# Gated cross attention with a Sinkhorn-mixed feed-forward: the output mask spread over the partitions by a product instead of a transfer, and three more chunks of mixing moved behind the last residual

## The chip, the cores and the metric

One Trainium2 chip, one core of it. The metric is the device time of one execution in microseconds (us). PE is TensorE, DVE is VectorE, ACT is ScalarE, POOL is GpSimd; SP's queue issues most of the transfers, ACT's queue some stores.

## The reference

The inputs are x and a context of shape (8, 512, 2048), 32-bit floats, and a mask of shape (8, 1, 2048) (all ones in the inputs drawn, but read by the kernel as data). The computation has two gated residual steps:

```
x = x + tanh(g_xattn) * xattn(layernorm(x), ctx, mask)
x = x + tanh(g_ffn)   * ffn(layernorm(x))

xattn: the 2048 columns are cut into 16 patches of 128 columns
  q, k = Wq, Wk @ layernorm(x) + bias      (256 x 128 per patch, 8 heads of 32)
  v    = Wv @ ctx + bias
  attn = softmax(q k / sqrt(32), masked)   within the patch
  o    = gelu(attn v)
  out  = (Wo @ o + bo) * mask

ffn: each row of 2048 is 4 streams of 512
  logits = rmsnorm(row) @ W.T + base       (24 of them: 16, 4 and 4)
  H_res  = 50 Sinkhorn iterations on the 4x4 matrix, mixed with the identity by a gate
  H_pre, H_post = softmax of 4 each
  y      = (sum_n H_pre[n] stream[n]) @ W_branch
  out[i] = sum_j H_res[i, j] stream[j] + H_post[i] * y
```

The mask multiplies the whole output of the attention, the bias `bo` included. The kernel uses that Wo is linear: it multiplies the mask into `o` ahead of Wo, and adds mask times `bo` as one more product.

## The kernel before

**Blocks and steps.** A batch has 512 rows; its 2048 columns are cut into 4 blocks of 512 columns, 32 blocks over the 8 batches. A block is 4 patches, and the loop runs over patches, `t` from 0 to 131, with `n = t // 4` the block. In each step a string, `ORDER`, gives the order in which parts are put into the program: `e` exponentials, `a` attention times v, `g`, `o` and `O` the output of the block before (`outp`), `p` and `P` the q/k projection of two blocks ahead, `s` scores and their maxima, `v` the v projection, `S` the statistics, `M` mixing. The program is written for a scheduler that lays out each engine's instructions by the order in which they are written (an earlier place is a higher priority) and by when their inputs and buffers come free in its own model of time; so an instruction can stand ahead of where it was written if its inputs are ready, and then the order on each engine is fixed.

**The output of a block (`outp`).** Its first part applies the gelu to `o` (L665, ACT, between two loads of an activation table, L665 and L667), loads the mask of the block's columns to all 128 partitions (`mb`, L669, one transfer of 256 KB on SP's queue with a single row as source, in a pool with one buffer), and multiplies `o` by it on POOL (L670). The second part transposes `o` on PE (L679), copies (L680), and forms the products that the logits need (L683); loads six rows of the mask's parts to `MR` (L691); and splits `o` into a high and a low part (`gh` L693 on ACT, `gl` L695 on POOL). The third part forms Wo times `o` in four row groups of 128 (L705 to L707), each closed by the product that adds mask times bias:

```python
T.matmul(ps, bo6[:, cs], mr, start=False, stop=True)
```

and adds the residual (L709, DVE), a sum of squares (L711, ACT), and a store of the new x to the tensor `x1s` in HBM (L712).

**The mask in three parts.** A 32-bit float is the sum of three bf16 numbers, each the rounded rest of the one before (`split3`). The mask's three parts and the bias's three parts stand in six rows each, `mrow_d` (and from it the two tiles `MR`, filled with zeros below the six rows) and `bo6`, paired so that the product over the rows gives the six leading terms of mask times bias.

**The chain of a batch.** When a batch's four blocks are done, `rawmap` and `ffn` make its logits and run the Sinkhorn iterations, 49 sweeps of small instructions (L882 to L892) that alternate between DVE and POOL (for the last batch DVE alone). For batches that have chunks on PE, `ffn` also writes small tensors to HBM and reads them back in another layout: `rec` (L834, L836) and `HR` (L923, L925).

**Two forms of mixing.** A batch's output is made in four chunks of 128 rows. `mixv` does a chunk on ACT, DVE and POOL: it loads the four streams (L953), forms the branch input (L958, L962, L963), transposes it and multiplies by W_branch on PE (L943 to L945), and for each of the four output streams adds up scaled streams (L981, L985, L986, L988) and the branch (L991), with a store on SP's queue (L992). `mixp` does a chunk by products: it loads the same rows interleaved (L1009), adds the mean on ACT (L1011), forms the branch input with a block-diagonal weight `PD` (L1012), transposes, multiplies by W_branch (L943 to L945 again, to `yp`), and forms the outputs by two products each with weights built on POOL from `post` and `HR` (`QD`, L1035 and L1036; L1046 and L1047), ending in a copy on ACT (L1049) and a store on ACT's queue (L1050).

The table `PE_MIX` says which chunks of each batch take the second form. Chunks of the first form go to the queue `mixq`, which is worked off within the loop, 3.25 steps of a chunk's 13 per loop step, from 30 steps after the batch's chain was written; batch 4's from t = 113 on. Chunks of the second form go to `tailq`, which is written behind the whole loop, so behind the residual of block 31. Before the change `tailq` holds 12 chunks: one of batch 4, four each of batches 5 and 6, three of batch 7.

**Buffers around the change.** `mb` has one buffer. `MR` are two tiles, taken in turn. PSUM is three pools of two buffers each: `ps_s` for scores, `ps_p` for projections, v, Wo and parts of `mixp`, `ps_t` (tag `t`) for attention times v, transposes, statistics and branch results.

Of the kernel before, what the change touches and what calls it, by code (L numbers as in the profile page):

```python
# [9 lines left out]
F32 = mybir.dt.float32  # L10
F32R = mybir.dt.float32r
F16 = mybir.dt.float16
BF16 = mybir.dt.bfloat16
# [6 lines left out]
P = 128  # L20
# [5 lines left out]
BLK = 512  # L26
# [48 lines left out]
D_OUT = 0  # L75
D_ST = 0
BUF_XP = 10
PE_MIX = ((), (), (), (), (3,), (0, 1, 2, 3), (0, 1, 2, 3), (1, 2, 3))
SPLITS = (1, 1, 1, 1, 1, 1, 1, 1)
CHAINS = ((0,), (1,), (2,), (3,), (4,), (5,), (6,), (7,))  # L80
BUF_SK = 2
# [17 lines left out]
def gated_xattn_mhc_kernel(  # L99
# [21 lines left out]
    V, A, G, T, SY = nc.vector, nc.scalar, nc.gpsimd, nc.tensor, nc.sync  # L121
# [6 lines left out]
    def ctile(shape, dt, name):  # L128
        return const.tile(shape, dt, tag=name, name=name)
# [27 lines left out]
    bor = ctile([3, 512], F32R, "bor")  # L157

    bo6 = ctile([P, 512], BF16, "bo6")
    MR = [ctile([P, BLK], BF16, f"MR{i}") for i in range(2)]  # L160
    cs3 = ctile([3, 2], F32, "cs3")
    base_t = ctile([P, NM], F32, "base_t")
# [10 lines left out]
    mrow_d = dram.tile([6, B * S], BF16, tag="mrow_d", name="mrow_d")  # L173
# [22 lines left out]
    ps_t = ctx.enter_context(tc.tile_pool(name="ps_t", bufs=2, space=PSUM))  # L196
# [166 lines left out]
    with tc.tile_pool(name="set", bufs=1) as st:  # L363
# [7 lines left out]
        def split3(parts, a, shape, name):  # L371

            left = stile(shape, F32, name)
            V.tensor_copy(parts[:, 0, :], a)
            V.tensor_tensor(left, a, parts[:, 0, :], ALU.subtract)
            V.tensor_copy(parts[:, 1, :], left)
            V.tensor_tensor(parts[:, 2, :], left, parts[:, 1, :], ALU.subtract)
# [97 lines left out]

        mh = stile([B * 16, 3, P], BF16, "mh")
        split3(mh, mkt, [B * 16, P], "mks")
        for r, t in enumerate((0, 0, 1, 0, 1, 2)):
            SY.dma_start(mrow_d[r : r + 1, :].rearrange("o (k w) -> (o k) w", w=P), mh[:, t, :])
        mT = ptile(B * 16, "mT")  # L480
        T.transpose(mT, mkt, ident[: B * 16, : B * 16])
# [23 lines left out]
        with ExitStack() as behind:  # L505
            for i in last.values():
                behind.enter_context(tc.issue_after(i.ins))

            wo = stile([P, 2, 512], F32, "wo", "w2")
            SY.dma_start(wo, woT.rearrange("(c p) d -> p c d", p=P))  # L510
            V.tensor_scalar(wo, wo, tgx, None, ALU.mult)
            A.copy(WoH, wo)
            V.tensor_tensor(WoL, wo, WoH.bitcast(F32), ALU.subtract)
            bo32 = stile([1, 512], F32, "bo32")
            SY.dma_start(bo32, bo.rearrange("(o e) -> o e", o=1))
            V.tensor_scalar(bo32, bo32, tgx[0:1, :], None, ALU.mult)
            boh = stile([1, 2, 512], F32R, "boh")
            V.tensor_copy(boh[:, 0, :], bo32)
            V.tensor_tensor(boh[:, 1, :], bo32, boh[:, 0, :].bitcast(F32), ALU.subtract)
            for t, r in ((0, 0), (1, 1), (0, 2)):  # L520
                SY.dma_start(brow_d[r : r + 1, :], boh[:, t, :].bitcast(F32))
            SY.dma_start(bor.bitcast(F32), brow_d)
            bo3 = stile([1, 3, 512], BF16, "bo3")
            split3(bo3, bo32, [1, 512], "bos")
            for t in [bo6] + MR:
                V.memset(t, 0.0)
            for r, t in enumerate((0, 1, 0, 2, 1, 0)):
                SY.dma_start(bo6[r : r + 1, :], bo3[:, t, :])


            V.memset(Wm, 0.0)
            V.memset(Wm[:, :, NM : NM + 1], 1.0)
            SY.dma_start(Wm[:, :, 0:NM], wmT.rearrange("(c p) m -> p c m", p=P))
            ws = ps_t.tile([P, BLK], F32, tag="t", name="ws")
            for k in range(16):
                T.matmul(ws[:, 0:32], onesb, Wm[:, k, :], start=(k == 0), stop=(k == 15))
            A.copy(wsum, ws[:, :NM])
            SY.dma_start(base_t, base.partition_broadcast(P))

            V.memset(cs3[:, 0:1], 1.0)  # L540
            V.tensor_copy(cs3[:, 1:2], ident[0:3, 2:3])
            V.tensor_tensor(cs3[:, 0:1], cs3[:, 0:1], cs3[:, 1:2], ALU.subtract)


            wbr = stile([P, 4, 512], F32, "wbr", "w4")
            SY.dma_start(wbr, wb.rearrange("(c p) e -> p c e", p=P))
            wmx = stile([P, 1], F32, "wmx")
            V.tensor_reduce(wmx, wbr.rearrange("p c e -> p (c e)"), AX.X, ALU.max, apply_absolute_value=True)
            wms = ps_t.tile([P, BLK], F32, tag="t", name="wms")[:, 0:1]
            T.matmul(wms, onesb, wmx, start=True, stop=True)  # L550
            V.tensor_scalar(ibw, wms, 1e-18, 1.0 / W_CAP, ALU.max, ALU.mult)
            sbw = stile([P, 1], F32, "sbw")
            V.reciprocal(sbw, ibw)
            V.tensor_scalar(wbr, wbr, sbw, None, ALU.mult)
            A.copy(WbH, wbr)
            V.tensor_tensor(WbL, wbr, WbH, ALU.subtract)
# [103 lines left out]
    def outp(n):  # L660

        b, k = divmod(n, NBLK)
        o = ob.pop(n)
        for g in range(2):
            gi = A.activation(o[:, g], o[:, g], AF.Gelu, bias=bvc[:, g : g + 1])  # L665
        with tc.issue_after(gi.ins), tc.high_priority():
            A.preload_act_table_set(EXP_SET)  # L667
        mb = gp.tile([P, BLK], F32, tag="mb", name="mb")
        SY.dma_start(mb, mask[b, k * BLK : (k + 1) * BLK].partition_broadcast(P))  # L669
        G.tensor_tensor(o, o, mb.unsqueeze(1).broadcast_to([P, 2, BLK]), ALU.mult)  # L670
        j0 = n * NP
        gt_ = op_.tile([P, NP, DK + 1], F32, tag="gT", name="gT")
        G.tensor_copy(gt_[:, :, DK], maskT[:, j0 : j0 + NP])
        yield
        for q in range(2):
            pt = ps_t.tile([P, 2, 2, P], F32, tag="t", name="gTp")
            for j in range(2):
                for e in range(2):
                    T.transpose(pt[:, j, e, :], o[:, e, (2 * q + j) * P : (2 * q + j + 1) * P], ident)  # L679
            V.tensor_copy(gt_[:, 2 * q : 2 * q + 2, 0:DK], pt.rearrange("p j e s -> p j (e s)"))  # L680
        g4 = ps_t.tile([P, DK + 1], F32, tag="t", name="g4")
        for p in range(NP):
            T.matmul(g4[32 * p : 32 * p + 32, :], Wm[:, k * NP + p, :], gt_[:, p, :], start=True, stop=True)  # L683
        if k == 0:
            g4s = lnp.tile([P, DK + 1], F32, tag="g4s", name="g4s", bufs=2)
            V.tensor_copy(g4s, g4)
            G4[b] = g4s
        else:
            V.tensor_tensor(G4[b], g4, G4[b], ALU.add)
        mr = MR[n % 2]  # L690
        SY.dma_start(mr[0:6, :], mrow_d[:, n * BLK : (n + 1) * BLK])  # L691
        gh = gp.tile([P, 2, BLK], F32R, tag="gh", name="gh")
        A.copy(gh, o)  # L693
        gl = gp.tile([P, 2, BLK], F32R, tag="gl", name="gl")
        G.tensor_tensor(gl, o, gh.bitcast(F32), ALU.subtract)  # L695
        if k == 0:
            sq2[b] = lnp.tile([P, 4, NBLK], F32, tag="sq2", name="sq2")
            x1s[b] = x1d.tile([D, S], F32, tag="x1s", name="x1s")
        xt = xtile.pop(n)
        yield  # L700
        for c in range(4):
            ps = ps_p.tile([P, BLK], F32, tag="p", name="op")
            cs = slice(c * P, (c + 1) * P)
            for e in range(2):
                T.matmul(ps, WoH[:, e, cs], gh[:, e], start=(e == 0), stop=False)  # L705
                T.matmul(ps, WoH[:, e, cs], gl[:, e], start=False, stop=False)  # L706
                T.matmul(ps, WoL[:, e, cs], gh[:, e], start=False, stop=False)  # L707
            T.matmul(ps, bo6[:, cs], mr, start=False, stop=True)  # L708
            V.tensor_tensor(xt[c], ps, xt[c], ALU.add)  # L709
            jk = fp.tile([P, BLK], BF16, tag="ph", name="junk2", bufs=BUF_PH)  # L710
            A.activation(jk, xt[c], AF.Square, bias=nmean[b][:, c : c + 1], accum_out=sq2[b][:, c, k : k + 1])  # L711
            defer(D_X1, "x1", lambda cs=cs, c=c: SY.dma_start(x1s[b][cs, k * BLK : (k + 1) * BLK], xt[c]))  # L712
            yield
# [39 lines left out]
    def ffn(bs):  # L753

        NT = 4 * len(bs)
        b = bs[-1]
        pe_mix = [PE_MIX[q - B] or PE_IN[q - B] for q in bs]
        tg = ""
# [170 lines left out]
    def mix(b, maps):  # L929
        E, cst, pre, prc, post, rec, HR = maps  # L930
        for c in range(4):
            if c in PE_IN[b - B]:
                yield from mixp(b, c, maps, True)
            elif c not in PE_MIX[b - B]:
                yield from mixv(b, c, maps)
# [148 lines left out]
    def act(c, t):  # L1084
# [55 lines left out]
        elif c == "O":  # L1140
# [3 lines left out]
            if n >= 1 and p == 3:  # L1144
                at("outp", run, og_[0])
                bb_, kk_ = divmod(n - 1, NBLK)
                if kk_ == NBLK - 1:
                    at("raw", rawmap, bb_)
                    p0 = tc.cur_priority
                    for grp in CHAINS:  # L1150
                        if grp[-1] == bb_ - B + 8:
                            grp = [q + B - 8 for q in grp if q + B - 8 >= 0]
                            res = at("chain", ffn, grp)
                            for q, maps in zip(grp, res):
                                mixq.append((t + LAGS[bb_], mix(q, maps)))
                                for c_ in PE_MIX[q - B]:
                                    tailq.append(mixp(q, c_, maps))
# [11 lines left out]

    nl = len(tailq) - len(PE_MIX[-1])  # L1170

# [62 lines left out]
```

## Time and profile before

| | before |
|---|---|
| median of 3 runs | 1668.7 us (1663.1 to 1676.0) |
| profiled execution | 1677.35 us, span 1675.5 us |
| PE busy | 1477.9 us (88%) |
| DVE busy | 1194.7 us (71%) |
| ACT busy | 1065.9 us (64%) |
| POOL busy | 821.3 us (49%) |
| granted PE clock, mean | 0.958 |
| HBM | 226.7 MB read, 101.2 MB written |

The profile is of one execution; a line number is that of the kernel before. "Busy" counts the time in which at least one instruction runs on the engine. PE's products overlap one another, so the mean time of a single product is longer than the time by which the next one follows. Where a view says what an engine waited for, it names the instruction whose end released it. Block 27's mask product (L670) starts at 1322.7, block 31's, the last, at 1478.9; the last residual's product is issued at 1491.9, and the first product of `mixp` at 1493.6.

### The profile page before, as it was taken

The numbers are of one execution on the slowest core, as the hardware profiler recorded it, in microseconds if no ns is written. First come the engines' busy times: TensorE is split into PE (matmuls) and PEld (weight loads), VectorE is DVE, ScalarE is ACT, GpSimd is POOL, SyncE is SP. The second block draws the span as 40 slices with busy tenths as digits, with TensorE's granted clock in tenths as the row PEclk, the third lists the DMA queues.
The fourth block names the chain that finished last, engine by engine and source line by source line (L and its number), as shares of the span: only waits on it lengthen the run. The fifth ranks groups of instructions, "written<-read, shape, count | busy, mean of one in ns | idle before, by whom it ended". The sixth has DMA issues, their size and how long they took to land.

```text
span 1675.5 us, 31675 instructions
## 1 busy us (share of the span) xinstructions
PE 1477.9 (88%) x10517; PEld 882.5 (53%) x10517; DVE 1194.7 (71%) x3552; ACT 1065.9 (64%) x1930; POOL 821.3 (49%) x1158
## 2 busy tenths in 40 slices
PE   4898999999999888889898898889889989789897
PEld 2544556656656554555555555555555556543333
DVE  7443434665776578777886789877988788877865
ACT  3357366767666766677578766687667767555454
POOL 2321323545454455546565745666667644643212
PEclk8999999999999999999899999999999989799999
DMA  5689786677678755886688765886567665234353
GB/s 190 172 240 256 236 268 194 188 236 247 173 209 236 228 168 178 233 256 195 177 241 252 227 188 165 245 251 190 183 173 212 193 176 145 98 122 152 109 169 122
DMA packets 257410, 330.53 MB, mean 197 GB/s; under 512 B 43543, under 2 KB 143191, under 8 KB 257246
## 3 DMA queue, kind: packets, MB, share of 16 engines
q1 hardware_dynamic: 249038, 315.59, 63.8%
q10 hardware_dynamic: 8208, 12.92, 2.1%
q8 instruction: 83, 1.36, 0.3%
q14 instruction: 81, 0.66, 0.1%
HBM read 226.71 MB, written 101.16 MB: 196 GB/s over the span
## 4 chain that ended last, share of the span: by engine, by line
PE 34%; DMA 20%; DVE 18%; ACT 11%; issue 8%; POOL 7%; SPq 1%; ACTq 0%; POOLq 0%; DVEq 0%
PE vp L336 4%; DMA xs<-in_x_dram 4%; DVE w L988 4%; DMA xTt<-in_xT_dram 3%; DMA QK<-qd 3%; PE qk L288 2%; PE qk L289 2%; PE op L705 2%; PE qk L290 2%; DMA out_dram<-w 2%; DVE smax L349 2%; PE op L706 2%; DMA xc<-x1s 2%; DMA x<-x1s 2%; PE smax L346 2%
## 5 line engine op out<-in xcount | busy, mean ns | idle before, releaser
L336 PE MATMUL vp<-Wv,ct 128*128 128x256 f32 x1024 | 249.8, 398 | 19.0 <-ACT VF L337 9.7
L336 PEld LDWEIGHTS vp<-Wv,ct 128*128 128x128 f32 x1024 | 201.6, 200 | 55.0 <-ACT VF L337 12.8
L888 POOL TENSOR_TENSOR W<-E,uv 128x64 f32<-128x64 f32 x343 | 117.8, 348 | 196.3 <-DVE uv L886 100.6
L288 PE MATMUL qk<-xh,WqkH 128*128 128x512 f16 x512 | 196.9, 385 | 8.9 <-DVE ev L295 6.0
L349 DVE TENSOR_REDUCE smax<-smax 128x8 f32<-128x1024 f32 x128 | 155.8, 1217 | 64.8 <-PE smax L346 62.8
L276 POOL TENSOR_TENSOR xl<-xn,xh 128x512 f16<-128x512 f32 x126 | 155.2, 1232 | 93.3 <-ACT xh L274 87.4
L988 DVE SCALAR_TENSOR_TENSOR w<-x,Et,w 128x512 f32<-128x512 f32 x180 | 181.4, 1009 | 26.4 <-POOL w L986 16.3
L289 PE MATMUL qk<-xl,WqkH 128*128 128x512 f16 x512 | 196.7, 384 | 3.9 <-POOL xl L276 3.9
L290 PE MATMUL qk<-xh,WqkL 128*128 128x512 f16 x512 | 196.3, 383 | 0.0
L882 POOL TENSOR_TENSOR W<-E,uv 128x64 f32<-128x64 f32 x308 | 106.9, 352 | 176.1 <-DVE uv L892 80.2
L635 ACT ACTIVATE e<-sT,ebi,esc 128x1024 f32<-128x1024 f32 x128 | 153.2, 1197 | 35.4 <-PE sT L633 35.0
L271 POOL TENSOR_SCALAR xn<-xt,ln_r,nb 128x512 f32<-128x512 f32 x126 | 109.3, 868 | 112.2 <-DMA xt<-in_x_dram 51.9
L890 DVE TENSOR_REDUCE sm<-W 128x16 f32<-128x64 f32 x392 | 98.6, 255 | 71.0 <-POOL W L888 67.5
L705 PE MATMUL op<-gh,WoH 128*128 128x512 f32 x256 | 118.6, 465 | 24.3 <-DVE ev L295 11.4
L711 ACT ACTIVATE junk<-xt,nmean 128x512 bf16<-128x512 f32 x128 | 91.6, 715 | 74.1 <-DVE xt L709 38.7
L294 ACT ACTIVATE ev<-qk,bqs 128x512 f16<-128x512 f32 x128 | 86.4, 677 | 73.3 <-PE qk L290 72.8
L295 DVE SCALAR_TENSOR_TENSOR ev<-qk,bqs,ev 128x512 f16<-128x512 f32 x128 | 93.6, 732 | 44.0 <-ACT ev L294 43.6
L346 PE MATMUL smax<-QK 97*128 97x128 f16 x1024 | 83.8, 224 | 40.9 <-DMA QK<-qd 28.7
L884 DVE TENSOR_REDUCE sm<-W 128x16 f32<-128x64 f32 x352 | 73.0, 211 | 60.2 <-POOL W L882 57.0
L709 DVE TENSOR_TENSOR xt<-op,xt 128x512 f32<-128x512 f32 x128 | 86.9, 679 | 38.9 <-PE op L708 38.4
L986 POOL TENSOR_TENSOR w<-w,pj 128x512 f32<-128x512 f32 x60 | 82.0, 1366 | 51.4 <-ACT pj L985 27.5
L706 PE MATMUL op<-gl,WoH 128*128 128x512 f32 x256 | 104.9, 410 | 0.0
(288 smaller groups left out, 3468.7 us busy)
## 6 DMA issues: line engine op xcount, KB each, us to landing
xt<-in_x_dram SPq DMA_DIRECT2D x64, 512.0 KB
ct<-in_cx_dram SPq DMA_DIRECT2D x64, 512.0 KB
qd<-ev SPq DMA_DIRECT2D x128, 256.0 KB
QK<-qd SPq DMA_DIRECT2D x64, 512.0 KB
xTt<-in_xT_dram SPq DMA_DIRECT2D x64, 512.0 KB
x1s<-xt SPq DMA_DIRECT2D x128, 256.0 KB
xs<-in_x_dram SPq DMA_DIRECT2D x56, 512.0 KB
x<-x1s SPq DMA_DIRECT2D x40, 512.0 KB
```

Of the source, the lines that this page charges most:

```text
L276: (V if n == 0 and c > 1 else G).tensor_tensor(l, xn, h, ALU.subtract)
L288: T.matmul(ps, WqkH[:, c, ms], hs[c], start=(c == 0), stop=False)
L289: T.matmul(ps, WqkH[:, c, ms], ls[c], start=False, stop=False)
L290: mm = T.matmul(ps, WqkL[:, c, ms], hs[c], start=False, stop=(c == 3))
L336: T.matmul(ps[:, h, :], ct[:, c, h * P : (h + 1) * P], Wv[:, c, :], start=(c == 0), stop=(c == 3))
L346: T.matmul(sc[:, h, :], q[0:97, h, sl], kk[0:97, h, sl], start=True, stop=True)
L349: V.tensor_reduce(mx, sc, AX.X, ALU.max)
L635: A.activation(e32, sc, AF.Exp, bias=ebi[:, t : t + 1], scale=esc[:, t : t + 1])
L705: T.matmul(ps, WoH[:, e, cs], gh[:, e], start=(e == 0), stop=False)
L706: T.matmul(ps, WoH[:, e, cs], gl[:, e], start=False, stop=False)
L888: (G if SK_POOL(b - B + 8) else V).tensor_tensor(W4[:, h], E4[:, h], ub[:, h], ALU.mult)
L988: V.scalar_tensor_tensor(w, x1[j], E[:, n, 4 * j + i : 4 * j + i + 1], w, ALU.mult, ALU.add)
```

## The change

The transfer of the mask to `mb` goes. The mask's six rows, `MR`, are loaded at the top of the block's output instead of further down, and a product with a weight `sel3`, ones in its first three rows and zero elsewhere, adds the first three rows up on every partition; ACT copies the result from PSUM to `mb`. For this the rows are set in another order: the first three are now the three parts of the mask, and the rows of the bias are exchanged to match, so that the product with `bo6` has the same six pairs. In `PE_MIX` batch 4 has all four chunks in the second form, where it had one.

```diff
-PE_MIX = ((), (), (), (), (3,), (0, 1, 2, 3), (0, 1, 2, 3), (1, 2, 3))
+PE_MIX = ((), (), (), (), (0, 1, 2, 3), (0, 1, 2, 3), (0, 1, 2, 3), (1, 2, 3))
...
+    sel3 = ctile([P, P], BF16, "sel3")
...
-        for r, t in enumerate((0, 0, 1, 0, 1, 2)):
+        for r, t in enumerate((0, 1, 2, 0, 0, 1)):
             SY.dma_start(mrow_d[r : r + 1, :].rearrange("o (k w) -> (o k) w", w=P), mh[:, t, :])
...
-            for t in [bo6] + MR:
+            for t in [bo6, sel3] + MR:
                 V.memset(t, 0.0)
-            for r, t in enumerate((0, 1, 0, 2, 1, 0)):
+            V.memset(sel3[0:3, :], 1.0)
+            for r, t in enumerate((0, 0, 0, 1, 2, 1)):
                 SY.dma_start(bo6[r : r + 1, :], bo3[:, t, :])
...
         mb = gp.tile([P, BLK], F32, tag="mb", name="mb")
-        SY.dma_start(mb, mask[b, k * BLK : (k + 1) * BLK].partition_broadcast(P))
+        mr = MR[n % 2]
+        SY.dma_start(mr[0:6, :], mrow_d[:, n * BLK : (n + 1) * BLK])
+
+        pm = ps_t.tile([P, BLK], F32, tag="t", name="pm")
+        T.matmul(pm, sel3, mr, start=True, stop=True)
+        A.copy(mb, pm)
         G.tensor_tensor(o, o, mb.unsqueeze(1).broadcast_to([P, 2, BLK]), ALU.mult)
...
-        mr = MR[n % 2]
-        SY.dma_start(mr[0:6, :], mrow_d[:, n * BLK : (n + 1) * BLK])
         gh = gp.tile([P, 2, BLK], F32R, tag="gh", name="gh")
```

## The prediction

> **What bounds the kernel now.** I read the page first, then the busy time by stage, then who waits around the mask, and last PE's own idle gaps.
>
> ```profile
> span 1675.5 us, 31675 instructions
> PE 1477.9 (88%) x10517; PEld 882.5 (53%) x10517; DVE 1194.7 (71%) x3552; ACT 1065.9 (64%) x1930; POOL 821.3 (49%) x1158
> ```
>
> PE is the busiest engine, but an average over unlike stages says little. In the next view each line is one stretch (start:end, length), then busy time of PE, PEld, DVE, ACT and POOL, the granted clock, the DMA share and GB/s. The first three run from one mask product to that four blocks later; the last is the tail behind the last residual.
>
> ```profile
> 414.15:570.92 156.77, 149.50 (x1204) 94.74 (x1203) 107.76 (x374) 105.05 (x197) 76.10 (x131) 0.99 0.70 207
> 1009.80:1200.17 190.37, 165.45 (x1256) 104.87 (x1255) 159.53 (x448) 134.48 (x244) 122.89 (x167) 0.95 0.70 210
> 1200.17:1382.07 181.90, 161.64 (x1231) 101.64 (x1229) 152.51 (x426) 126.21 (x230) 116.12 (x161) 0.96 0.64 187
> 1493.60:1675.50 181.90, 159.90 (x502) 59.86 (x501) 128.85 (x529) 90.80 (x165) 48.90 (x94) 0.98 0.45 143
> ```
>
> Four blocks without mixing take 156.8 us with PE busy 95% of it; four blocks with one batch (four chunks) mixed take 190.4 us, PE busy 87%. So one chunk mixed inside the loop costs (190.4 - 156.8) / 4 = 8.4 us, although its own PE work is far less; the rest is PE waiting on DVE, ACT and POOL, and a lower granted clock (0.95 against 0.99). The third stretch, also with four chunks but hardly any statistics, gives (181.9 - 156.8) / 4 = 6.3 us.
>
> The tail is PE's: twelve chunks of `mixp`, one of `mixv`. Only 22 us of its 181.9 are idle on PE. From 1541.20 to 1576.37, the copies of three successive branch results, PE was busy 35.17 of 35.17 us, so a chunk costs 11.7 us of PE there. The waits that PE has in the tail and in the last blocks (in brackets, with what ended them):
>
> ```profile
> 1420.39 1.70 PE L679 MATMUL gTp<-ident,o 128*128 128x128 f32 x8 [3.31 <-POOL o L670]
> 1449.98 0.61 PE L633 MATMUL sT<-QK 99*128 99x128 f16 x8 [2.24 <-ACT e L635]
> 1458.90 1.97 PE L679 MATMUL gTp<-ident,o 128*128 128x128 f32 x8 [8.32 <-POOL o L670]
> 1481.28 1.97 PE L679 MATMUL gTp<-ident,o 128*128 128x128 f32 x8 [6.41 <-POOL o L670]
> ...
> 1590.50 3.78 PE L1047 MATMUL mx<-xc,QD 128*128 128x512 f32 x4 [6.57 <-POOL QD L1036]
> ...
> 1648.82 1.98 PE L1047 MATMUL mx<-xc,QD 128*128 128x512 f32 x4 [1.80 <-POOL QD L1036]
> ```
>
> The last two are PE waiting for the Sinkhorn results of batches 6 and 7 (HR, read by L1036). The first, third and fourth are PE waiting for the mask product L670. Its tile `mb`:
>
> ```profile
> L669 SPq DMA_DIRECT2D mb<-in_mask_dram x32: 333/378/1156, 96.9 to 1458.9; - x32
> L670 POOL TENSOR_TENSOR o<-o,mb x32: 2333/2354/2808, 120.6 to 1478.9; 128x1024 f32<-128x1024 f32 x32
> its engine sat idle before it (us, times) until:
>   ACT o L665: 47.4, 22
> who waited for it (us, times):
>   PEld gTp L679: 22.3, 8
>   PE gTp L679: 20.5, 5
> ```
>
> What POOL waited for before L670 was always the gelu (L665), never the mask's transfer. That transfer is hidden; taking it away shortens no wait of L670.
>
> **The change, part by part.**
>
> *Mixing taken out of the loop.* Batch 4's chunks 0 to 2 leave `mixv`. One chunk is 9 L988 (180/20) at 1.009, 4 L991 at 0.916 and one split at 0.670: 13.4 us of DVE; 0.80 + 6 x 0.714 + 4 x 0.806 + 2 copies at 0.57 = 9.5 us of ACT; 3 x 1.321 + 3 x 1.366 = 8.1 us of POOL; on PE 12 products at the 0.215 us by which such products follow each other, and 4 transposes at 0.11, 3.1 us. Its two loads and four stores leave SP's queue too. What reaches the end lies between 3 x 3.1 = 9.3 us (PE work alone) and 3 x 8.4 = 25 us (the stage's price). The chunks start at 1328.4, 1378.5 and 1423.6 (L958) and end by 1460, so they lie over blocks 28 to 30, where the latency gaps at 1449 to 1482 stay in part with or without mixing. With the stage's lower price, 3 x 6.3 = 19, near the middle: **-20**.
>
> *The same chunks on PE, in the tail.* Each is 8 L1012, 16 L1046/L1047, 4 transposes and 12 products on PE, 7.3 us of ACT, 0.7 of DVE, 2.6 of POOL, 2 loads on SP and 4 stores on ACT's queue. Three at 11.9 (a little over the 11.7 above, since the start of the tail ran slower) are 36 us. The tail had waits that the chunks now fill: eight chunks of batches 4 and 5 instead of five stand ahead of batch 6, so its HR is there, 6.57 + 1.80 = 8.4 us off. Chain 7 ends at 1643 and must not become late: the tail starts some 20 us earlier, batch 7's second halves come 36 - 20 = 16 us later than now. Bounds: 3 x 11.7 - 8.4 = 27 and 3 x 13.0 = 39 (159.9 busy less the `mixv` chunk, over twelve, nothing filled). I take **+28**.
>
> *The mask on PE.* 32 products of 128x512 bf16. The nearest row is L708, 128 of the same shape at 0.399 us each from start to end, following each other by about 0.22: 7.0 us if PE is the bound everywhere, 12.8 if nothing overlaps. In the stage without mixing PE idles 5%, so it costs its full 0.22; with mixing a part falls into waits. **+5**. It takes one of two `ps_t` buffers until ACT has copied it; PE's waits for that pool were about 1 us in all (L650), so nothing more. `sel3` is two memsets at about 0.3 us in the setup, behind loads: nothing.
>
> *The copy to `mb` on ACT.* 32 copies of 128x512 from PSUM; L1015, the same shape, takes 0.585: 18.7 us on an engine 64% busy that holds 11% of the chain that ended last, so 11% of it, **+2**; bounds 0 and 18.7. `mb` has one buffer, so the copy waits for the L670 of the block before, at least 22 us earlier, and stands ahead of whatever ACT has next. The mask rows `MR` (L691) were and are loaded two blocks ahead: that of block 31 at 1436.5, 42 us before its L670, so the moved load is hidden; without that cover it would cost a landing of 2 to 3 us a block, as on `HR` in the chain of waits (2.63).
>
> *The transfer removed.* 32 x 262 KB = 8.4 of 330.5 MB, 2.5% of the traffic, and 32 issues of 0.378 us on SP's queue, where the next in line are `ct` and `qd`. PE waited 28.7 us for `QK`, 13.9 for `xTt`, 7.0 for `ct`; 2.5% of 49.6 is 1.2 us, and at 230 GB/s one mask takes 1.1 us, so if every one of these 30 waits had one ahead it would be 33. **-2**, bounds 0 and -33, near the first since L669 often goes out with no such wait behind it.
>
> Sum: -20 + 28 + 5 + 2 - 2 = **+13 us**. The profiled execution took 1677.35 us (span 1675.5); it lies 0.5% above the median of 1668.7 and just above the runs' 1663.1 to 1676.0. Against the median: 1668.7 + 13 = **1682 us**, 0.8% slower. About 1% is what a measurement of this kernel can tell from no change.
>
> **Rule against trace.** The copy uses ACT behind a gelu that is wrapped in two table loads. The trace has each at 1283 ns (L665 and L667), and the next activation starts at once: the load of 1476.18 ends with the gelu at 1477.48. The Trainium skill, "ScalarE: Activation LUTs", section "What ACT_TABLE_LOAD costs", states the same load but a drain of about 1380 ns on top, 2.66 us for a switch. No drain shows here; by the rule the second rival below would be an estimated 1.4 us a block dearer, by the trace it is not.
>
> **Rivals.**
>
> 1. *The moved chunks fill the loop's gaps (ends on the other side).* PE's four waits from 1420 to 1482 are 3.31 + 2.24 + 8.32 + 6.41 = 20.3 us. With four chunks of batch 4 ready by then, their first products could stand in them: 1682 - 20 = **1662**. For it: the one such chunk of before had its rows loaded and biased by 1375 (L1011) and its PD made at 1034. Against: its first product still ran only at 1493.6, right behind the last residual, past all four gaps. It decides if L1012 appears ahead of the last L705.
>
> 2. *The mask's copy stands behind the gelu.* If ACT's order has the copy behind gelu and the second table load, L670 starts 1.283 + 0.585 = 1.9 us later in a block. Over 32 blocks that is 60 us; POOL waited for the gelu in 22, PE for L670 in 5 (8 with weight loads), so some ten blocks pass it on: +20, **1702**. For it: L670 is what PE waits for most at the end. Against: the copy needs nothing of this block's attention and can go early.
>
> 3. *The loop gives back only the PE work.* If blocks 28 to 30 are held by their own latencies, 9 instead of 20: **1693**. For it: PE is busy only 28 of 38.6 us in the block from 1417.88, DVE 33. Against: the price seen in both mixing stages.
>
> That the change does not do what it says would show as L988 still 180 times; nothing speaks for that.
>
> **How the numbers follow.** The sum: 0.47, with an own range of 1672 to 1694 (0.28 within 1%, 0.19 slower). Rival 1: 0.25 (0.13 faster, below 1652; 0.12 within). Rival 2: 0.18 (0.16 slower, 0.02 within). Rival 3: 0.10 (0.08 and 0.02). Together faster 0.13, same 0.44, slower 0.43. The range of 1655 to 1702 leaves out about one in ten on each side and takes in the unknown transfer gain as far as rival 1 carries it.
>
> **What would show it.** Right: L1012 120 times instead of 96, L988 153 and L991 68; the last residual 10 to 20 us earlier than 1493; a tail of about 210 us with no wait over 3 us for QD; 32 copies near 0.585 on ACT; PE waits for L670 not longer than 20 us. Wrong: moved chunks at work before the last residual, copies right behind the second table load, or a tail that still waits for batch 7.

## The result and the profile after

The changed kernel takes 1684.4 us in the median against 1674.8 of the kernel before on the same chip. The ratio over all runs is 1.0072, with a 95% interval of 1.0049 to 1.0094, so 12 us more (8 to 16); the two medians alone lie 10 apart. The forecast of +13 us is met in its total. It was put together wrongly: the mixing came out 24 us better than forecast and the mask about as much worse, as the experiments show.

The profiled execution after took 1675.0 us, near the fastest of its kernel, and that of before 1677.35 us, which lies above its kernel's median. The ends of the two traces therefore say nothing about the 12 us. What the traces can say is which stretch became shorter and which longer.

The page of the kernel after, first the lines that answer to the first fence of the prediction (PEld is PE's loading of weights, which overlaps its products):

```profile
span 1673.2 us, 31685 instructions
PE 1499.2 (90%) x10555; PEld 895.5 (54%) x10621; DVE 1158.7 (69%) x3515; ACT 1077.1 (64%) x1956; POOL 796.1 (48%) x1149
```

PE's busy time went up by 21.3 us (1477.9 to 1499.2) and DVE's went down by 36.0: the moved chunks left DVE and went to PE, as announced. The count of the mixing confirms it (a group of the page, and tiles): 153 additions of a stream instead of 180, 120 products with `PD` instead of 96, the first of them at 1475.4, right behind the last residual, whose last product starts at 1473.7 (1491.9 before).

```profile
L993 DVE SCALAR_TENSOR_TENSOR w<-x,Et,w 128x512 f32<-128x512 f32 x153 | 144.1, 943 | 21.0 <-POOL w L991 10.7
```
```profile
L1017 PE MATMUL xpp<-xc,PD x120: 592/604/617, 1475.4 to 1641.3; 128*32 128x512 f32 x120
```

Busy time by stretch of the kernel after, with the columns as in the prediction (start:end, length, busy PE, PEld, DVE, ACT, POOL, clock, DMA share, GB/s). The first line runs from block 27's mask product (now L677) to block 31's, the second is the tail:

```profile
1328.96:1460.10 131.14, 113.02 (x975) 76.92 (x981) 92.92 (x376) 79.67 (x156) 57.44 (x124) 0.94 0.44 122
1475.40:1673.20 197.80, 190.81 (x622) 73.42 (x621) 124.37 (x512) 110.65 (x197) 52.21 (x97) 0.99 0.51 163
```

The same four blocks before, from the same view of its trace:

```profile
1322.67:1478.89 156.22, 130.37 (x1041) 84.55 (x1038) 128.31 (x404) 103.38 (x194) 81.96 (x135) 0.90 0.52 155
```

The last four blocks went from 156.2 to 131.1 us (-25), the tail from 181.9 to 197.8 us (+16). In the tail PE was idle 181.9 - 159.9 = 22.0 us before and is idle 197.8 - 190.8 = 7.0 us now. Not all of that is waiting: PE's last product ended at 1670.6 before and ends at 1667.2 now, so 4.9 us of the first number and 6.0 of the second lie behind it, where the last results are copied and stored. Between its products PE waited 17.1 us in the tail before and waits 1.0 now. Its waits of more than two microseconds after 1405, from its timeline (in brackets); behind 1500 the timeline shows none of any length:

```profile
1440.43 0.80 PE L635 MATMUL sT<-QK 99*128 99x128 f16 x6 [4.35 <-ACT e L637]
...
1462.49 1.97 PE L686 MATMUL gTp<-ident,o 128*128 128x128 f32 x8 [6.94 <-POOL o L677]
```

So the late blocks gave 25 us and the tail took 16 back; these two stretches alone would make the kernel faster. What is lost lies ahead of them: block 27's mask product starts 6.3 us later than before (1329.0 against 1322.7). That points to the mask for the loss. Its tile `mb` in the kernel after:

```profile
L676 ACT COPY mb<-pm x32: 557/579/593, 120.2 to 1456.0; 128x512 f32<-128x512 f32 x32
L677 POOL TENSOR_TENSOR o<-o,mb x32: 2337/2350/2887, 125.5 to 1460.1; 128x1024 f32<-128x1024 f32 x32
its engine sat idle before it (us, times) until:
  ACT o L667: 78.4, 20
  ACT mb L676: 20.5, 3
```

The copy took 0.579 us, as costed, and POOL now waits for it 3 times, 20.5 us together, where it never waited for the mask before (the prediction shows the same view of before).

### The profile page after: what moved, and what is told of

Its sections match the earlier page's. It is cut to its first block, busy times and chain, and to the rows that moved or that the text cites. A ratio compares the mean times of both kernels' runs of the same rounds, so it can differ in the third digit from the quotient of the medians.

```text
span 1673.2 us, 31685 instructions
## 1 busy us (share of the span) xinstructions
PE 1499.2 (90%) x10555; PEld 895.5 (54%) x10621; DVE 1158.7 (69%) x3515; ACT 1077.1 (64%) x1956; POOL 796.1 (48%) x1149
## 4 chain that ended last, share of the span: by engine, by line
PE 45%; DMA 16%; DVE 15%; ACT 8%; issue 7%; POOL 7%; SPq 1%; POOLq 0%; another core or an unknown queue 0%; ACTq 0%; DVEq 0%
PE vp L337 6%; PE mx L1051 3%; PE qk L289 3%; PE mx L1052 3%; PE qk L290 3%; DMA xs<-in_x_dram 3%; PE qk L291 3%; DMA QK<-qd 3%; PE op L710 2%; DVE w L993 2%; DMA xTt<-in_xT_dram 2%; DMA out_dram<-w 2%; DVE smax L350 2%; POOL xl L277 2%; PE xpp L1017 2%
## 5 line engine op out<-in xcount | busy, mean ns | idle before, releaser
L893 POOL TENSOR_TENSOR W<-E,uv 128x64 f32<-128x64 f32 x343 | 115.2, 339 | 218.5 <-DVE uv L891 100.6
L289 PE MATMUL qk<-xh,WqkH 128*128 128x512 f16 x512 | 198.4, 388 | 5.6 <-DVE ev L296 3.5
L290 PE MATMUL qk<-xl,WqkH 128*128 128x512 f16 x512 | 198.4, 388 | 4.4 <-POOL xl L277 4.3
L887 POOL TENSOR_TENSOR W<-E,uv 128x64 f32<-128x64 f32 x308 | 105.8, 346 | 152.3 <-DVE uv L897 73.4
L993 DVE SCALAR_TENSOR_TENSOR w<-x,Et,w 128x512 f32<-128x512 f32 x153 | 144.1, 943 | 21.0 <-POOL w L991 10.7
L710 PE MATMUL op<-gh,WoH 128*128 128x512 f32 x256 | 117.9, 462 | 24.8 <-DVE ev L296 16.5
L677 POOL TENSOR_TENSOR o<-o,mb 128x1024 f32<-128x1024 f32 x32 | 75.7, 2365 | 105.0 <-ACT o L667 78.4
```

The lines of the kernel that those rows point to most:

```text
L289: T.matmul(ps, WqkH[:, c, ms], hs[c], start=(c == 0), stop=False)
L290: T.matmul(ps, WqkH[:, c, ms], ls[c], start=False, stop=False)
L887: (G if SK_POOL(b - B + 8) else V).tensor_tensor(W4[:, h], E4[:, h], vb[:, h], ALU.mult)
L893: (G if SK_POOL(b - B + 8) else V).tensor_tensor(W4[:, h], E4[:, h], ub[:, h], ALU.mult)
L993: V.scalar_tensor_tensor(w, x1[j], E[:, n, 4 * j + i : 4 * j + i + 1], w, ALU.mult, ALU.add)
```

## The experiments

Ratios are to the kernel before, timed in the same study; microseconds worked out from a ratio take 1674 us as 1. "The mask alone" is the change without its line on `PE_MIX`, "the mixing alone" is that line without the rest.

**The two halves, and the whole once more.** The changed kernel again, then each half by itself:

```diff
 # the mask alone: as the change, but
+PE_MIX = ((), (), (), (), (3,), (0, 1, 2, 3), (0, 1, 2, 3), (1, 2, 3))
 # the mixing alone: as before, but
+PE_MIX = ((), (), (), (), (0, 1, 2, 3), (0, 1, 2, 3), (0, 1, 2, 3), (1, 2, 3))
```

> The changed kernel once more, for a second profile of it and a ratio beside the others. Theory A (the prediction's sum: mask +5, mixing +8): ratio 1.005 to 1.009, last mask product near 1472 (6 to 10 later than in the first profile, since that execution took 1675 where the median is 1684), tail near 198. Theory B (the two traces: mixing gives 25 in the loop and costs 16 in the tail, so the mask must cost about 20): the same ratio, with block 27's mask product some 15 to 20 us later than before's 1322.7. Rival C (the two profiles stand, and the difference of the medians comes from the tail in other executions): block 27 at 1325 to 1330 and a tail of 205 or more.

Measured: 1.0073 (1.0042 to 1.0103). Its profile repeats the two stretches, 131.2 us for the four blocks and 197.8 for the tail, and block 27's mask product starts at 1334.7, 12 us later than before.

> The mask by product, PE_MIX as before. Theory A: +5 us, ratio 1.003. Theory B: +20 us, ratio 1.012. Rival C: ratio 1.000 to 1.004.

Measured: 1.0098 (1.0063 to 1.0134), +16 us.

> The mask by transfer as before, the three chunks moved. Theory A: +8 us, ratio 1.005. Theory B: -9 us, ratio 0.995, last mask product near 1454, tail near 198. Rival C: ratio 1.004 to 1.008.

Measured: 0.9902 (0.9866 to 0.9937), -16 us (the medians, 1661.6 and 1675.3, lie 14 apart). This kernel beats both the one before and the one after.

The sign of the whole is the sign of the mask. The mixing, forecast as +8 (-20 + 28), is a gain of 16; the mask, forecast as +5 (+5 + 2 - 2), costs 16 by itself (11 to 22). Within the whole it seems to cost more: the whole less the mixing alone is 1.0073 - 0.9902 = 0.0171, 29 us (21 to 36; 25 by the medians). The mixing alone in the same two stretches as above:

```profile
1316.85:1444.20 127.35, 113.06 (x984) 74.42 (x981) 96.33 (x372) 78.43 (x154) 57.74 (x122) 0.97 0.49 135
1458.70:1657.10 198.40, 191.03 (x622) 73.39 (x621) 127.44 (x512) 110.92 (x196) 52.77 (x97) 1.00 0.51 164
```

127.4 for the four blocks (-29) and 198.4 for the tail (+16.5): the two stretches are much as in the kernel after, without any change to the mask. In the built program of this kernel the first 8000 of PE's 12217 entries have the order of before.

**One chunk more.** If moved chunks are cheap because they fill the tail's waits, the next one should be dear: with the mixing alone PE's last product ends at 1651.4, so only 192.66 - 191.03 = 1.6 us of waits between products are left in its tail.

```diff
-PE_MIX = ((), (), (), (), (3,), (0, 1, 2, 3), (0, 1, 2, 3), (1, 2, 3))
+PE_MIX = ((), (), (), (3,), (0, 1, 2, 3), (0, 1, 2, 3), (0, 1, 2, 3), (1, 2, 3))
...
-            recs[j] = skp.tile([P, 16, 4], F32, tag="rec", name="rec", bufs=4)
+            recs[j] = skp.tile([P, 16, 4], F32, tag="rec", name="rec", bufs=5)
...
-                HR = skp.tile([P, 16, 4], F32, tag="HR", name="HR", bufs=4)
+                HR = skp.tile([P, 16, 4], F32, tag="HR", name="HR", bufs=5)
```

> The mix-only kernel with one more chunk moved behind the last residual, chunk 3 of batch 3 (with one more buffer for each of the two small tensors of PE mixing). If the three chunks came cheap because the tail had 15 us of PE waits to fill: a fourth costs about 12.5 in the tail and saves 6 to 10 in the loop, ratio to before 0.991 to 0.994, against 0.990 of mix-only. If a chunk in the tail is cheaper than 8 us whatever the waits: 0.988 or less.

Measured: 0.9983 (0.9958 to 1.0008), above the 0.991 to 0.994 expected. Three chunks gained 16 us, the fourth gives 13 or so of them back (6 to 21). Its tail:

```profile
1456.10:1667.80 211.70, 203.50 (x662) 78.24 (x661) 125.27 (x501) 117.66 (x207) 54.09 (x95) 1.00 0.52 163
```

The tail is 13.3 us longer than with three chunks, PE busy 12.5 of it, and idle 8.2 against 7.4: hardly anything was left to fill, so the chunk cost its whole time, as expected. The loop failed the expectation: the tail's start came only 2.6 us earlier (1456.1 against 1458.7), where 6 to 10 were expected. This chunk no longer pays.

**Is it the copy's place behind the gelu?** The mask of a block is loaded, multiplied and copied one block earlier, at the end of that block's first part, so that the copy is written ahead of the gelu in all blocks but one:

```diff
+    def spread(n):
+        mr = MR[n % 2]
+        SY.dma_start(mr[0:6, :], mrow_d[:, n * BLK : (n + 1) * BLK])
+        mbs[n] = gp.tile([P, BLK], F32, tag="mb", name="mb")
+        pm = ps_t.tile([P, BLK], F32, tag="t", name="pm")
+        T.matmul(pm, sel3, mr, start=True, stop=True)
+        A.copy(mbs[n], pm)
...
+        mb = mbs.pop(n)
...
+        if n + 1 < NTOT:
+            spread(n + 1)
```

> As the mask-only kernel, but the mask of a block is loaded, multiplied and copied where the block before ends its own, so that the copy stands ahead of the gelu on ScalarE in all blocks but one (in the changed kernel it stands behind the gelu and the second table load in seven of 32). If the late copies are what the mask costs: 1.9 us x 7 = 13 us less than mask-only at most, ratio 0.99 of it. Theory A, and a mask that costs through PE's and ScalarE's own time: within 0.2% of mask-only.

Measured: 1.009 (1.0063 to 1.0117), the same as the mask alone within 9 us. The copies behind the gelu are real: 7 of 32 in the kernel after and in the mask alone. In the timeline of ACT in the kernel after, the one of block 27 stands behind the second table load:

```profile
1324.95 1.34 ACT L667 ACTIVATE o<-o,bvc 128x512 f32<-128x512 f32 x2
1326.30 1.28 ACT L669 ACT_TABLE_LOAD   x1
1327.60 0.60 ACT L338 ACTIVATE VF<-vp 128x512 f32<-128x512 f32 x1
1328.09 0.58 ACT L676 COPY mb<-pm 128x512 f32<-128x512 f32 x1
```

With the early copy none stands behind its gelu, and POOL's waits for the copy (4 times, 22.4 us in the mask alone) are gone, yet the time stayed. So the late copies are not where most of the time goes, with the reserve that this kernel has a new order of its own, as is said below.

**Which part of the mask's path?** The transfer taken away without anything in its place (the mask of block 0 serves all blocks; the other 31 masks are left out of the computation); product and copy added while the transfer stays, the copy going to a tile that nobody reads; the product with a copy of one column; and the copy alone, from a constant:

```diff
 # no transfer: as before, but
+        if n == 0:
+            mb1.append(gp.tile([P, BLK], F32, tag="mb", name="mb"))
+            SY.dma_start(mb1[0], mask[b, k * BLK : (k + 1) * BLK].partition_broadcast(P))
+        mb = mb1[0]
 # both: as the mask alone, but with the transfer to mb, and
-        A.copy(mb, pm)
+        A.copy(ms, pm)
 # product: likewise, with
+        A.copy(ms, pm[:, 0:1])
 # copy: likewise, without pm, and
+        A.copy(ms, onesb[:, 0:1].broadcast_to([P, BLK]))
```

> The kernel before with the mask transferred once, for block 0, and that tile used for all blocks: what taking the 31 other transfers away is worth by itself. It leaves out the masks of blocks 1 to 31. Theory A (the mask costs by the time of its product and copy, the transfer was hidden): -2 us, ratio 0.997 to 1.001. Theory B (the loss lies in what the order of SP's queue becomes without the transfer): +8 to +16, ratio 1.005 or more.

Measured: 1.001 (0.9981 to 1.0039). The transfer was hidden; taking it away is worth nothing that this measures (-3 to +7 us).

> The kernel before with product and copy added, the copy going to a tile that nobody reads, and the transfer kept. Theory A: as mask-only plus the 1 to 2 us of the transfer, ratio 1.009 to 1.012. Theory B: 1.004 or less, since SP's queue keeps its transfer.

Measured: 1.023 (1.0189 to 1.027), +39 us.

> The kernel before with the product added, but only one of its 512 columns copied, and the transfer kept. Theory A with equal shares: 7 us for the products on PE, ratio 1.004. If PE alone carries the loss (its time, its clock, the PSUM buffer): 1.008 to 1.010. If ScalarE's copy carries it: 1.000 to 1.003.

Measured: 1.0151 (1.0115 to 1.0188), +25 us. This and the kernel with both lie above everything that was expected of them.

> The kernel before with only the copy added: 32 times 128x512 on ScalarE from a constant, to a tile that nobody reads, no product, the transfer kept, the rows of the mask loaded as early as in the changed kernel. Theory A with equal shares: ratio 1.004. If PE alone carries the loss: 1.000 to 1.002. If the copy does: 1.007 or more.

Measured: 1.0154 (1.0117 to 1.0191), +26 us.

With the transfer kept, product and copy together cost 2.3% and either of them 1.5%; with the transfer gone the same two cost 1.0%, though the transfer by itself is worth nothing. No fixed price for each part gives these numbers.

**The load's place, and the instructions' length.** Only the load of the six rows moved up, nothing added; and the mask alone with product and copy cut to 64 of 512 columns (the other 448 keep ones, so 7/8 of the mask is left out):

```diff
 # the rows' load: as before, but these two lines behind the transfer of the mask
+        mr = MR[n % 2]
+        SY.dma_start(mr[0:6, :], mrow_d[:, n * BLK : (n + 1) * BLK])
 # narrow: as the mask alone, with mb one tile set to ones, and
-        T.matmul(pm, sel3, mr, start=True, stop=True)
-        A.copy(mb, pm)
+        T.matmul(pm[:, 0:64], sel3, mr[:, 0:64], start=True, stop=True)
+        A.copy(mb[:, 0:64], pm[:, 0:64])
```

> The kernel before with one line moved: the six mask rows are loaded at the top of the block's output, as in the changed kernel, right behind the mask's transfer. No work is added or taken away. Theory A (the loss is the time of product and copy): ratio 0.998 to 1.002. Theory D (the loss is the scheduler's new order of all engines, which any such edit brings): 1.006 to 1.015, with block 11's mask product 10 us or more behind that of before, as in all the kernels with product or copy.

Measured: 0.9991 (0.9962 to 1.0019). The planner (the scheduler that lays out each engine's instructions) gave each engine the very order of before, the moved load included, so this was the kernel before run once more. That makes it a measure of two profiles of one program: spans of 1675.5 and 1666.4 us, 9 apart.

> The mask-only kernel with product and copy cut from 512 to 64 columns (the tile of the mask is set to ones once; it leaves out seven eighths of the mask): the same instructions, semaphores and buffers, about 0.03 instead of 0.22 us on PE and about 0.2 instead of 0.58 us on ScalarE for each block. Theory A: the loss falls from 1.0098 to 1.003 or less. Theory D, or a loss by the instructions being there at all: 1.007 or more.

Measured: 1.0146 (1.0113 to 1.0179), +24 us, with an eighth of the columns. The length of the added instructions is not what costs.

At this point I held that one more instruction in ACT's stream per block was the cause, whatever its length: every kernel that lost had one, and the two that had none lost nothing. But another thing goes with it. In the built programs the order of the engines' instructions is another in all kernels that lose: about 2000 of PE's 12217 entries are out of the order of before in the mask alone, and about as many with the product, with the copy, in the narrow one, with the early mask and with both. The added instructions made the planner lay out the program anew almost from its start. (It did so without the transfer too, with 1866 entries displaced, and that cost nothing; so a new order need not be worse.)

**The order of before, with the mask's path in it.** The last experiment keeps the two apart: the mask alone, but with each engine's instructions chained in the order that they have in the kernel before, by edges that set the order and are no waits. The 32 products and 32 copies go wherever the planner puts them in between.

```diff
+def pin(tc, nc, mybir):
...
+    for e, deltas in seq.items():
+        at, last = 0, None
+        for d in deltas:
+            at += d
+            i = key[e, at]
+            if last is not None:
+                tc.add_manual_dep(i, last.name, info, reason="pin")
+            last = i
...
         gated_xattn_mhc_kernel(tc, *args)
+        pin(tc, nc, _mybir)
```

> The mask by its product as in the kernel with the mask alone (ratio to before 1.0098), PE_MIX as before, but every instruction that the kernel before has stands on its engine exactly where it stood there: its order on each engine is written out and chained by edges that are no waits. Added are 32 products with their weight loads on PE and 32 copies on ACT, wherever the planner puts them into that fixed order; 32 transfers are gone from SP's queue. In the kernel with the mask alone some 2000 of PE's 12217 entries, 1050 of DVE's 3554 and 440 of ACT's 1805 stand elsewhere than before; in the kernel without the transfer about as many (1866, 974, 397) and it took 1.001; in the one with the rows' load alone moved none, so that one was the kernel before run once more (0.9991). Theory A, the new order: the mask costs because the planner lays the whole program out anew around the added instructions, and the orders it finds are worse; with the old order kept the loss goes, but for the products' own 32 x 0.22 = 7 us at most: ratio 0.998 to 1.004. Theory B, the instruction itself: 32 more instructions in ACT's and PE's streams cost about 0.5 us each through what waits behind them, whatever the order: ratio 1.008 to 1.013, and the last mask product again some 20 us later than before. A ratio of 1.004 to 1.008 would be a share of both.

Measured: 1.0046 (1.0017 to 1.0074), +8 us: between the two theories, a share of both. What is left is about what the products were costed at on PE (32 x 0.22 = 7 us); product and copy were not measured apart in this order. The other half of the mask's 16 us is gone with the new order. The difference of the two ratios is 0.0052, with an interval of 0.0007 to 0.0097 (root of the summed squares of the two), so the order's share lies anywhere between 1 and 16 us. My theory of the added ACT instruction fell as the whole explanation: the 32 copies are there, 6 of them still behind their gelu, POOL waits for them longer than in the mask alone (33.2 us against 22.4), and the kernel loses less. Its tile `mb`:

```profile
L678 ACT COPY mb<-pm x32: 556/574/592, 121.7 to 1474.7; 128x512 f32<-128x512 f32 x32
L679 POOL TENSOR_TENSOR o<-o,mb x32: 2339/2352/2796, 125.3 to 1478.3; 128x1024 f32<-128x1024 f32 x32
its engine sat idle before it (us, times) until:
  ACT mb L678: 33.2, 6
```

Where the order costs is seen in blocks 3 to 11, in which mixing starts only near the end (its first addition in the kernel after is at 523.7 us), from the mask product of block 3 to that of block 11. In the order of before: the kernel before, the rows' load, and the pinned kernel.

```profile
258.51:570.92 312.41, 297.32 (x2403) 190.63 (x2404) 199.52 (x659) 208.73 (x388) 144.98 (x230) 0.98 0.72 212
```
```profile
255.10:565.80 310.70, 297.64 (x2403) 190.72 (x2404) 199.49 (x659) 208.90 (x388) 144.62 (x230) 0.98 0.72 213
```
```profile
262.62:571.74 309.12, 298.27 (x2413) 189.21 (x2414) 205.69 (x659) 212.02 (x396) 145.09 (x231) 0.99 0.71 207
```

In new orders: the mask alone, the narrow one, and the one without the transfer, which adds no instruction at all.

```profile
259.40:585.20 325.80, 306.76 (x2419) 194.78 (x2420) 201.29 (x659) 212.74 (x399) 144.00 (x230) 0.97 0.68 198
```
```profile
262.40:590.80 328.40, 306.76 (x2421) 193.39 (x2420) 207.53 (x665) 210.46 (x398) 145.41 (x234) 0.97 0.67 197
```
```profile
263.90:583.70 319.80, 298.93 (x2389) 190.32 (x2406) 204.20 (x655) 210.23 (x389) 144.03 (x229) 0.98 0.69 200
```

The three with the old order take 309 to 312 us, the three with a new one 320 to 328, with the same work but for eight products and copies. The pinned kernel has these products too, at full width, and is the shortest of all six. The other traces fall the same way: 310.8 and 307.3 us with the mixing alone and with one chunk more, which have the old order here, and 321 to 332 with the change itself, the early mask, the product, the copy and both. PE is idle 10.9 us in the pinned kernel (309.12 - 298.27), 19.0 in the mask alone, 21.6 in the narrow one and 20.9 without the transfer (this trace misses some of PE's products). In the mask alone and in the narrow one PE is also busy 8.5 us longer than in the pinned kernel, so waits are only half of it there. The kernel without the transfer won the loss back over the next four blocks (its mask product of block 15 came 2.0 us later than before, that of block 11 12.8 later) and ended even; the mask alone was as near at block 15 (+2.3) and then lost again, to +22 at block 27. So the loss is neither a fixed price per block nor in one place: it is made of local gains and losses of an order.

Over the whole profile the mask alone and the pinned kernel differ in PE's busy time, and hardly in its idle time (194.2 and 192.4 us), with the same products:

```profile
PE 1502.0 (89%) x10549; PEld 896.4 (53%) x10549; DVE 1197.9 (71%) x3554; ACT 1081.2 (64%) x1962; POOL 821.7 (48%) x1158
```
```profile
PE 1482.9 (89%) x10549; PEld 883.3 (53%) x10549; DVE 1202.7 (72%) x3554; ACT 1080.0 (64%) x1962; POOL 822.2 (49%) x1158
```

The mean granted clock was 0.947 in the first and 0.959 in the second; over all their executions it was 0.952 and 0.956, and 0.955 and 0.956 for the kernel before beside them. So part of what the new order costs goes with a lower clock; which of the two brings the other was not tested.

Two things stay open. Which displaced instructions make the stretches longer wasn't traced. And whether and why the mask costs more beside the mixing (29 us against 16, a difference of 2 to 22) wasn't tried: the whole change with the order kept was not run.

## Why the prediction was right in the sum and wrong in two terms

- **Mixing taken out of the loop, -20.** Right in its direction, a little small in its size. The last four blocks became 25 us shorter in the kernel after and 29 in the mixing alone, at the upper bound of 25 that I had from the first mixing stage, or above it. I took a middle value because the latency gaps of blocks 28 to 30 would stay in part; they did: PE's idle time in the four blocks went from 25.9 to 18.1 us (156.22 - 130.37, 131.14 - 113.02). The greater part came from PE's busy time, which fell by 17.4, above the 9.3 that I took for the chunks' products (12 x 0.215 + 4 x 0.11 is 3.0 a chunk, so 9.1).
- **The same chunks in the tail, +28.** This term failed, by 12: the tail grew by 15.9, below my lower bound of 27. Two sizes were off. PE's busy time in the tail rose by 30.9 us, 10.3 a chunk and not 11.9; the granted clock of the whole tail rose too (0.98 to 0.99), and the fourth chunk, with the clock at 1.00 on both sides, cost 12.5, so 10.3 is not a chunk's own price. And 16.1 us of PE's waits were filled (17.1 to 1.0), where I counted only the two named waits for QD, 8.4. The prediction read 22 us of idle time and used none of it but these two; 17.1 of the 22 were waits between products. With those filled the low bound would have been 3 x 11.7 - 17.1 = 18, and 15.9 lies below it by the smaller cost of a chunk.
- **The products, +5, the copies, +2, the transfer, -2.** With the order of before kept, these three cost 8 us (3 to 12) against the 5 forecast, so their sum was right within the noise; the three sizes were not measured apart in that order. The transfer alone, in a new order of its own, was worth nothing that can be measured (1.001). Its far bound of 33 was too far: the waits for `QK`, `xTt` and `ct` are 14, 9 and 1 in the trace of before, so 24 and not 30.
- **The term that was missing.** The sum held every instruction and no order. The layout of all engines is planned anew for each version of the program, and here that cost about 9 us more (1.0098 against 1.0046; 1 to 16). The kernels that added only part of the mask's path and lost 24 to 26 us suggest that it can be more; they were not run in the old order. I wrote in the account of the kernel that an instruction can stand ahead of where it was written and that the order is then fixed, and priced nothing for it.
- **Rival 1** (chunks in the loop's gaps) did not happen by its own test: the first product with `PD` ran at 1475.4, behind the last residual. Yet its direction, a gain by the mixing, was right by another way: the chunks filled the tail's waits, not the loop's.
- **Rival 2** (the copy behind the gelu) was seen in 7 blocks and POOL waited for the copy, 20.5 us; with all copies early the time was the same within 9 us (1.009 against 1.0098), so the +20 did not show.
- **Rival 3** (only the PE work given back) is refuted: 25 us, not 9.
- **What would show it.** 120 products with `PD` and 153 stream additions, the last residual 18 us earlier, copies at 0.579 us, PE's products waiting 13.8 us for the mask product, no wait over 3 us for QD: as said. The tail was 198 us long where about 210 was said, which is the failed term.
- **The rule on table loads** ("ScalarE: Activation LUTs", "What ACT_TABLE_LOAD costs" in the Trainium skill) adds some 1380 ns of drain to the load. In the timeline above the second load takes 1.28 us from 1326.30, and the next activation starts at 1327.60, right behind it: there is no room for such a drain.

So +13 was met by luck, because two errors cancel: the mixing came out better than forecast by about 24 us (-16 against +8), and the mask, beside the mixing, worse by about 24 (29 against 5).

## What to carry to other kernels

Where work is moved to a stage, its cost there is its own time less the bounding engine's waits that it fills, small ones included (not the idle time behind the engine's last instruction), and only once they are used up does each further piece cost in full: three chunks made the tail 16 us longer, the fourth 13 by itself. Where a planner lays out fixed orders, a change of a few instructions can come with a new order of everything else, and is then priced together with it: measure the halves apart, and before a small loss is blamed on an instruction, put it into the old order. A comparison of two profiles of one execution each is good for stretches (blocks 3 to 11 differed by 1.7 us between two profiles of one program); their ends differed by 9 us.

## What was unexpected of the hardware

The granted clock changed with the layout. In the last four blocks it was 0.90 before, 0.94 in the kernel after and 0.97 with the mixing alone, in the lines above, where PE was idle 25.9, 18.1 and 14.3 us. Of the 29 us that the four blocks gained with the mixing alone, PE's busy time gives 17.3 (130.37 to 113.06), about 8 more than the chunks' own products by my count of 9.3. That the shorter waits brought the higher clock is a guess from these three rows; no run tests it.

An added instruction's own time was a poor guide: 32 products with copies of one column each cost 25 us in one order (with the transfer kept), 32 products with full copies 8 us in another (without it).
